# Feeding TensorE values of the chain between the layers of a four-layer graph network

## The chip, the cores and the metric

The kernel runs on one core of one Trainium2 chip, as one launch; the host only transposes some inputs. The metric is the device time of the launch in microseconds. The engines are TensorE (PE in the profile, its weight loads PEld), VectorE (DVE), ScalarE (ACT), GpSimd (POOL) and SyncE (SP), which issues most DMAs. Each runs its own queue of instructions in order; they wait for one another through semaphores.

## What is computed

A graph of N = 2708 nodes with D = 128 features passes through four layers over one dense-stored adjacency matrix `adj` (2708 x 2708, float32, some 2.4% of it not zero). Each layer adds its output to its input and normalizes the rows:

```python
x = _layernorm(x + _L0_gnn_ref(x, adj, ...))       # messages gelu(s_i + d_j + b), weighted by adj; update; layernorm
x = _layernorm(x + _L1_gnn_ref(x, adj, adj, ...))  # sigmoid gates of q k^T, times adj twice; update; layernorm
x = _layernorm(x + _L2_gnn_ref(x, adj, ...))       # hyperbolic: distances of all pairs, attention, exp and log maps
x = _layernorm(x + _L3_gnn_ref(x, adj, ...))       # swish(adj x W + b), twice
```

All arithmetic that matters here is in float32. A float32 matmul is two passes of PE, so two weight loads and two matmul records in the profile.

## The kernel before, in words

Rows of x are kept in 22 tiles of 128 rows (the last has 20), as `x[128, 22, 128]` in SBUF. The four layers follow one another, and each depends on all rows of the one before it.

**Layer 0** (to 880 us) works through blocks of neighbours: PE picks their messages (L817, L822), ACT takes the gelu (L895), DVE weighs (L882), PE adds up (L833). The order is written out by hand under `manual_schedule`, which keeps every engine's instructions in the order of the program. Its tail is what the change touches: `U.sums(n)` multiplies a group of four tiles by the update weights (L863), DVE adds the rest (L864), ACT takes the gelu (L865); `U.rows(n)` adds x (L870) and takes statistics (`moments`, L208). When n is 2, the eight last `far_sum` steps run: DVE adds eight weighted tiles into one tile `extra`, in place (L795). Then `U.norm.all(between)` normalizes twice: `begin` computes mean and scale of 11 tiles from the statistics (`normalizer`, small values of 11 columns), and `shift` applies them on ACT (L246); `add` scales h in place on DVE (L265), adds x (L266) and takes statistics again; `end` shifts x. This goes in two runs of 11 tiles, `early` and `late`; `between` does the last two groups of layer 0, of one tile each.

**Layer 1** (to 1175 us) makes transposed products first (L1042 to L1067), then gates and sums for all pairs of tiles (L1098 to L1105), then an update by groups, then `norm.all_but_end()`: both `begin`, both `add`, and the normalizer of all 22 tiles, whose shift is left to later layers.

**Layer 2** prepares (L1186 to L1298): PE transposes x (L295) and multiplies it (L1211); then comes a long chain on values of 128 x 22, one number for each row of x, made by the helper class `Values` (`tt`, `ts`, `act`, `recip`; L140 to L161); from its results ACT and DVE build X (L1260, L1261), PE transposes it (L1263) and further tables (L1289). This part isn't under `manual_schedule`: the scheduler of the framework orders it by the order of the program and by when operands are ready. Then come all pairs of tiles in trios (L1335 to L1393), for two halves of the columns.

**The end of layer 2 and layer 3** are again written out by hand. `end(1)` and `end(0)` finish layer 2 for tiles 11 to 21 and 0 to 10, each a chain of DVE and ACT with small values of 11 columns and 128-column steps (`each`, L1513). Both take their transposes first; then end(1) runs to its end, then end(0). Layer 3's `neighbours` multiplies x by rows of the adjacency matrix (L1634), first the 11 tiles of end(1), beginning with tile 21 of 20 rows, so PE works while end(0) runs. A second `neighbours` on the result ends the kernel.

Before and after these places PE has real work; within them it waits for DVE and ACT. PSUM has eight banks; the pools of layer 0 (`p_misc`, `p_slot`, `p_out`) take all, and layer 2's preparation takes seven.

Of the kernel before, what the change touches and what calls it, by code (L numbers as in the profile page):

```python
# [20 lines left out]
P = 128  # L21
# [18 lines left out]
def gnn_stack(ctx: ExitStack, tc: tile.TileContext, t, out: bass.AP):  # L40
# [64 lines left out]
    def groups():  # L105
# [4 lines left out]
        return g  # L110

    class Values:

# [24 lines left out]
        def tt(self, a, b, op):  # L138
            o = self.new(a)
            nc.vector.tensor_tensor(o, a, b, op=op)  # L140
            return o

# [6 lines left out]
        def ts(self, a, s1, op0, s2=None, op1=ALU.bypass):  # L149
            o = self.new(a)  # L150
            nc.vector.tensor_scalar(o, a, s1, s2, op0=op0, op1=op1)
            return o

        def act(self, a, func, **kw):
            o = self.new(a)
            nc.scalar.activation(o, a, func, **kw)
            return o

        def recip(self, a):
            o = self.new(a)  # L160
            nc.vector.reciprocal(o, a)  # L161
            return o

# [41 lines left out]
    def moments(st, src, a, b):  # L205

        for i in range(a, b):
            nc.vector.bn_stats(out=st[:, i, :], in_=src[:, i, :])  # L208

    def normalizer(st, a, b, V, sq=None, into=None):  # L210


        even, odd, m2, m5 = (st[:, a:b, k] for k in (1, 4, 2, 5))

        def stt(in0, scalar, in1, op0, op1):
            o = V.new(in0)
            nc.vector.scalar_tensor_tensor(o, in0, scalar, in1, op0=op0, op1=op1)
            return o


        d = V.tt(even, odd, ALU.subtract)
        q = stt(d, 1.0 / 16.0, d, ALU.mult, ALU.mult)
        if sq is None:
            m = stt(m2, LN_EPS * D, m5, ALU.add, ALU.add)
            w = stt(m, 0.25 / D, q, ALU.mult, ALU.add)
        else:
            m = V.tt(m2, m5, ALU.add)
            var = stt(m, 0.25 / D, q, ALU.mult, ALU.add)
            w = V.ts(var, 0.25 * LN_EPS, ALU.add)

        root = V.act(w, AF.Sqrt)
        both = V.tt(even, odd, ALU.add)
        r, off = into or (V.new(d), V.new(d))
        nc.vector.reciprocal(r, V.add(root, V.mul(w, V.recip(root))))
        nc.vector.scalar_tensor_tensor(off, both, -0.5, r, op0=ALU.mult, op1=ALU.mult)
        if sq is not None:
            nc.vector.scalar_tensor_tensor(sq[:, a:b], var, 4.0 * D, V.mul(r, r), op0=ALU.mult, op1=ALU.mult)
        return r, off

    def shift(dst, src, a, b, by, turns="va"):  # L240

        r, off = by
        for i in range(a, b):
            c = slice(i - a, i - a + 1)
            if turns[i % len(turns)] == "a":
                nc.scalar.activation(dst[:, i, :], src[:, i, :], AF.Identity, bias=off[:, c], scale=r[:, c])  # L246
            else:
                nc.vector.tensor_scalar(dst[:, i, :], src[:, i, :], r[:, c], off[:, c], op0=ALU.mult, op1=ALU.add)

    def normalize(dst, src, st, a, b, V, sq=None):  # L250
        shift(dst, src, a, b, normalizer(st, a, b, V, sq))

    class Resnorm:
# [18 lines left out]
        def all(self, between=lambda: None):  # L272
# [4 lines left out]
            self.begin(*late)  # L277
            self.end(*early, "v")
            self.add(*late)
            self.end(*late)  # L280

# [137 lines left out]
    with ExitStack() as l0:  # L419
# [10 lines left out]
        with ExitStack() as msg:  # L430
# [174 lines left out]
            class Rows:  # L605
# [183 lines left out]
                def far_sum(self, k):  # L789
# [4 lines left out]
                    else:  # L794
                        nc.vector.scalar_tensor_tensor(self.extra, f, w, self.extra, op0=ALU.mult, op1=ALU.add)  # L795

                def turn(self):
# [82 lines left out]
            with tc.manual_schedule():  # L880
# [34 lines left out]
                for n in range(ahead):  # L915
# [5 lines left out]
                    if n == 2:  # L921
                        for step in far_sums:
                            step()
                for step in last_turn:
# [21 lines left out]

                U.norm.all(between)

# [67 lines left out]
    def layers_1_to_3(top, before_end=lambda: None):  # L1016

        with ExitStack() as l1:
# [55 lines left out]
            with ExitStack() as att:  # L1074
# [49 lines left out]
                with tc.manual_schedule():  # L1124
# [24 lines left out]
                    look(len(banks) - 1)  # L1149
                    norm.all_but_end()  # L1150

# [9 lines left out]
        with ExitStack() as l2:  # L1161
# [27 lines left out]
            with ExitStack() as pre:  # L1189
# [18 lines left out]
                for n, (a, b, r) in enumerate(together):  # L1208
# [4 lines left out]
                    for i in range(a, b):  # L1213
                        nc.vector.bn_stats(out=st[:, i, :], in_=M[:, i, :D])
                My, Ml, Mr = (M[:, :, D + k] for k in range(3))
                yy, yl, yr = (yw[:, k:k + 1] for k in range(3))
# [253 lines left out]
        with ExitStack() as l3:  # L1470
# [27 lines left out]
            def end(hf):  # L1498
# [11 lines left out]
                def each(dst, src, v, other):  # L1510

                    for i in range(n):
                        nc.vector.scalar_tensor_tensor(dst[:, i, :], src[:, i, :], v[:, i:i + 1], other[:, i, :],  # L1513
                                                       op0=ALU.mult, op1=ALU.add)

                def squares(src):
# [103 lines left out]

            def neighbours(src, order, have, at_end, then, meanwhile, when=0):


                acc = [pacc.tile([P, b - a], F32, name=f"acc{k}") for k, (a, b) in enumerate(banks)]
                swish = Swish(acc, then)
# [47 lines left out]
            with tc.manual_schedule():  # L1673
                nc.sync.dma_start(out=VT0, in_=v_tab)
                for j in near1 + near0:
                    kept[j] = fetch(j, held.tile([P, N], F32, name=f"held{j}"))
                ends = [end(1), end(0)]
                for e in ends:
                    next(e)
                for e in ends:  # L1680
                    for _ in e:
                        pass

                def more():
# [5 lines left out]
                assert sorted(order) == list(range(NT))  # L1690
                first = neighbours(x, order, kept, 3, keep, more, len(far1 + near1) - 1)
                back = (far1 + far0)[::-1]
# [44 lines left out]
```

## Time and profile before

| | |
|---|---|
| device time, three runs | 1918.69, 1918.76, 1921.46 us (median 1918.76) |
| span of the profiled execution, first to last instruction | 1917.7 us |
| PE, DVE, ACT, POOL busy | 1659.6, 1542.7, 1132.0, 680.1 us |
| mean granted TensorE clock | 0.930 |
| matmul records, weight loads | 13973, 13973 |
| last sums of layer 0 to first gates of layer 1 | 880.6 to 955.3 us |
| last update of layer 1 to layer 2's last table | 1171.5 to 1242.6 us |
| last sums of layer 2 to first product of layer 3 | 1615.6 to 1672.4 us |

The profile is of one execution, whose own time lies about 1 us over its span. "PEclk" is the clock that the throttle granted to TensorE, 1.00 being full speed. A timeline row gives start, duration, engine, line, operation, output and inputs, the shape, how many instructions were merged into the row, and in brackets the engine's idle time before it with what ended it. A window's row gives, for each engine, its busy time and the number of its instructions in that stretch, then the clock, the share of the DMA engines and their GB/s. A busy PE is one with a matmul in flight; it says nothing of how much of the array works.

### The profile page before, as it was taken

Reading aid. Unit: us, or ns where it says so; the run is one execution under the profiler, and the core shown is the slowest. Engines: PE = TensorE matmul, PEld = TensorE weight load, DVE = VectorE, ACT = ScalarE, POOL = GpSimd, SP = SyncE. Lnnn points to the kernel's source line nnn. Section 1 sums busy time; section 2 is a strip of 40 time slices with the busy share of each in tenths; the row PEclk is TensorE's granted clock in tenths of the full one; section 3 lists DMA queues with packets and bytes.
Section 4 is the critical chain, followed back from the end, with each engine's and each line's share of the span. In section 5 each row is a group of like instructions: output and inputs, shape, how many; then the busy total and the mean of one; then the engine's idle time right before and its main releaser. Section 6 shows DMA issues by size and latency. Waiting matters only on the chain.

```text
span 1917.7 us, 36464 instructions
## 1 busy us (share of the span) xinstructions
PE 1659.6 (87%) x13973; PEld 949.3 (50%) x13973; DVE 1542.7 (80%) x3632; ACT 1132.0 (59%) x1581; POOL 680.1 (35%) x426
## 2 busy tenths in 40 slices
PE   5899999999999999885699996689998996199995
PEld 4666666666666666664444443322222322044542
DVE  7899999999999999986588885789999997760104
ACT  3566666667666666654344444599998994440003
POOL 5667757767766776664100000022000243000000
PEclk8899999999999999997799997779998997599997
DMA  8756566665666666443044410122222212453330
GB/s 223 161 117 148 121 140 143 132 143 119 148 127 133 146 128 142 91 103 109 1 151 149 170 63 1 61 91 91 78 80 70 98 63 120 161 203 145 139 127 31
DMA packets 218839, 223.63 MB, mean 117 GB/s; under 512 B 28389, under 2 KB 204875, under 8 KB 212067
## 3 DMA queue, kind: packets, MB, share of 16 engines
q1 hardware_dynamic: 167614, 197.53, 33.1%
q0 software_dynamic: 51040, 23.68, 10.5%
q8 instruction: 111, 1.82, 0.4%
q14 instruction: 74, 0.60, 0.1%
HBM read 213.33 MB, written 7.83 MB: 115 GB/s over the span
## 4 chain that ended last, share of the span: by engine, by line
DVE 37%; PE 32%; POOL 10%; issue 7%; ACT 7%; DMA 6%; SPq 0%; DVEq 0%; ACTq 0%; POOLq 0%
PE acc L1634 10%; POOL far L781 9%; PE lg L1098 5%; PE acc L1105 5%; DVE ix L777 5%; DMA far<-d_tab,ix 3%; DVE w L1375 3%; DVE u L1361 3%; DVE m L1364 3%; DVE W L882 3%; PE sl L817 2%; DVE extra L795 2%; DVE m L1381 2%; DVE o L739 2%; DVE m L1378 2%
## 5 line engine op out<-in xcount | busy, mean ns | idle before, releaser
L781 POOL DMA_INDIRECT far<-d_tab,ix x352 | 562.3, 1597 | 259.5 <-DVE W L882 110.8
L895 ACT ACTIVATE g<-sl 128x768 f32<-128x768 f32 x484 | 393.4, 813 | 259.0 <-PE sl L822 240.5
L817 PE MATMUL sl<-dA,S 124*128 124x153 f16 x4840 | 409.0, 232 | 10.4 <-DVE W L882 8.0
L817 PEld LDWEIGHTS <-S 124*128 124x128 f16 x4840 | 331.0, 98 | 80.0 <-issue 68.4
L833 PE MATMUL acc<-g,W 128*32 128x128 f32 x4840 | 206.2, 278 | 0.5 <-DVE W L882 0.5
L1335 POOL TENSOR_TENSOR at<-at,off 128x128 f32<-128x128 f32 (+1 forms) x22 | 71.2, 3249 | 328.8 <-DMA at<-in_adjT 301.2
L833 PEld LDWEIGHTS acc<-g,W 128*32 128x32 f32 x4840 | 140.9, 109 | 58.7 <-issue 54.6
L822 PE MATMUL sl<-s,same 50*128 50x384 f16 x968 | 162.0, 308 | 0.0
L1391 PE MATMUL accV<-m,X 128*128 128x512 f32 (+4 forms) x264 | 128.4, 628 | 33.5 <-DVE m L1381 29.1
L882 DVE TENSOR_TENSOR W<-sl,own 128x150 f32<-128x150 f32 x484 | 143.1, 299 | 14.5 <-ACT g L895 14.2
L1099 ACT ACTIVATE w<-lg,row_L_gnn_gate_bias 128x512 f32<-128x512 f32 (+1 forms) x132 | 83.5, 636 | 108.2 <-PE lg L1098 106.9
L1343 PE MATMUL ps<-XT 128*128 128x512 f32 (+4 forms) x264 | 143.9, 629 | 3.8 <-ACT m L1348 3.6
L707 DVE TENSOR_SCALAR S<-rk 124x1000 f16<-124x1000 bf16 (+1 forms) x330 | 133.4, 430 | 0.0
L777 DVE FIND_INDEX8 ix<-v,o 128x8 uint32<-128x2728 f32 x44 | 131.7, 2993 | 0.0
L316 DVE TENSOR_TENSOR g<-ps,row_L_gnn_b 128x512 f32<-128x512 f32 (+2 forms) x14 | 7.9, 574 | 148.3 <-PE ps L314 148.2
L1098 PE MATMUL lg<-qT,mT 128*128 128x512 f32 (+2 forms) x264 | 121.1, 547 | 3.6 <-ACT w L1099 3.1
L1105 PE MATMUL acc<-w,both 128*128 128x512 f32 (+2 forms) x264 | 121.2, 547 | 0.0
L795 DVE SCALAR_TENSOR_TENSOR extra<-far,v,extra 128x128 f32<-128x128 f32 x330 | 114.8, 348 | 6.3
L739 DVE SCALAR_TENSOR_TENSOR o<-ps,ar 128x496 f32<-128x496 f32 x132 | 82.4, 624 | 38.1 <-PE ps L728 31.7
L1634 PE MATMUL acc<-at,x 128*128 128x512 f32 (+2 forms) x156 | 66.2, 574 | 48.8 <-ACT x L246 48.8
L1100 DVE TENSOR_TENSOR w<-w,at 128x512 f32<-128x512 f32 (+1 forms) x132 | 82.5, 625 | 27.2 <-ACT w L1099 27.1
L1391 PEld LDWEIGHTS accV<-m,X 128*128 128x128 f32 (+1 forms) x264 | 52.1, 211 | 97.0 <-issue 57.7
(358 smaller groups left out, 2697.6 us busy)
## 6 DMA issues: line engine op xcount, KB each, us to landing
at<-in_adjT SPq DMA_DIRECT2D x42, 1354.0 KB
ar<-in_adj SPq DMA_DIRECT2D x105, 248.0 KB
far<-s_tab SPq DMA_DIRECT2D x44, 512.0 KB
at<-in_adjT SPq DMA_DIRECT2D x42, 448.0 KB
at<-in_adjT SPq DMA_DIRECT2D x21, 704.0 KB
at<-in_adjT SPq DMA_DIRECT2D x21, 650.0 KB
held<-in_adjT SPq DMA_DIRECT2D x7, 1354.0 KB
at<-in_adjT SPq DMA_DIRECT2D x21, 280.0 KB
```

The lines of the kernel that those rows point to most:

```text
L777: nc.vector.max_index(ix, self.v[:, n * 8:n * 8 + 8], self.o.rearrange("p b j -> p (b j)"))
L781: nc.gpsimd.indirect_dma_start(out=self.far[n][:, k, :], out_offset=None, in_=d_tab[:, :], in_offset=bass.IndirectOffsetOnAxis(ap=self.ix[ ...
L795: nc.vector.scalar_tensor_tensor(self.extra, f, w, self.extra, op0=ALU.mult, op1=ALU.add)
L817: nc.tensor.matmul(group[c], self.S[h][:, n, c, :], dA[q][:, b, c, :], start=c % 3 == 0 and q == 0, stop=False)
L822: nc.tensor.matmul(out, same[p], self.s3[p, :e - a, :], start=False, stop=True)
L833: nc.tensor.matmul(self.acc[q:q + 32, k, :], W[:, c, :], g[:, c, :], start=b == 0 and k == 0, stop=ends)
L882: nc.vector.tensor_tensor(W[:, :, :RG].rearrange("p (k c) i -> p k c i", k=2), columns_of(sl, D, DA), own[:, None, None, :].to_broadcast([ ...
L895: nc.scalar.activation(g.rearrange("p (k c) d -> p k c d", k=2), columns_of(sl, 0, D), AF.Gelu, scale=1.0 / D_SCALE)
L1098: nc.tensor.matmul(lg, mT[:, j * P:j * P + r], qT[:, a:b], start=True, stop=True)
L1105: nc.tensor.matmul(acc[k], mrow[:rows[j], j, :], ws[j][:rows[j], a:b], start=j == 0, stop=j == NT - 1)
L1391: nc.tensor.matmul(accV[:, a:b], X[:self.r, self.j, :], self.m[:, a:b], start=first, stop=last)
L1634: nc.tensor.matmul(acc[k], src[:rows[j], j, :], at[:rows[j], a:b], start=j == order[0], stop=j == order[-1])
```

## The change

A helper `touch(o)` follows most small steps: if a scratch place is open, PE multiplies the 128 x 128 identity by the value just made, into PSUM that nobody reads. `awake(ps)` opens such a place for a stretch of the program; `awake(None)` closes it for one. Nothing that the output needs is changed. A touch reads its value, so what later writes the same place must wait until the touch is done, and it stands in PE's queue where the program puts it.

```diff
@@ helpers
+    scratch = []
+
+    @contextmanager
+    def awake(ps):
+        scratch.append(ps)
+        yield
+        scratch.pop()
+
+    def touch(o):
+        if scratch and scratch[-1] is not None:
+            nc.tensor.matmul(scratch[-1][:, :o.shape[1]], ident, o, start=True, stop=True)
+        return o
@@ class Values: tt, ts, act and recip
-            return o
+            return touch(o) if len(o.shape) == 2 else o
@@ moments
             nc.vector.bn_stats(out=st[:, i, :], in_=src[:, i, :])
+            touch(st[:, i, :])
@@ normalizer: stt
-            return o
+            return touch(o)
@@ shift
+            touch(dst[:, i, :])
@@ Resnorm.all
             between()
             self.begin(*late)
-            self.end(*early, "v")
-            self.add(*late)
-            self.end(*late)
+            with awake(None):
+                self.end(*early, "v")
+                self.add(*late)
+                self.end(*late)
@@ far_sum
                         nc.vector.scalar_tensor_tensor(self.extra, f, w, self.extra, op0=ALU.mult, op1=ALU.add)
+                    touch(self.extra)
@@ tail of layer 0
                     if n == 2:
-                        for step in far_sums:
-                            step()
+                        with awake(p_out.tile([P, PB, D], F32, name="acc")[:, 0, :]):
+                            for step in far_sums:
+                                step()
...
-                U.norm.all(between)
+                with awake(p_out.tile([P, PB, D], F32, name="acc")[:, 0, :]):
+                    U.norm.all(between)
@@ tail of layer 1
-                    norm.all_but_end()
+                    with awake(acc[0][:, :P]):
+                        norm.all_but_end()
@@ layer 2, after the products of x and to the end of its preparation
+                psum_t = pre.enter_context(tc.tile_pool(name="ps_pre2t", bufs=1, space=PSUM))
+                pre.enter_context(awake(psum_t.tile([P, P], F32, name="scratch")))
@@ each, in end(hf)
                         nc.vector.scalar_tensor_tensor(dst[:, i, :], src[:, i, :], v[:, i:i + 1], other[:, i, :],
                                                        op0=ALU.mult, op1=ALU.add)
+                        if i % 2:
+                            touch(dst[:, i, :])
@@ before layer 3
+                acc = sums_of()
                 ends = [end(1), end(0)]
                 for e in ends:
                     next(e)
-                for e in ends:
-                    for _ in e:
-                        pass
+                with awake(acc[0][:, :P]):
+                    for _ in ends[0]:
+                        pass
+                for _ in ends[1]:
+                    pass
...
-                first = neighbours(x, order, kept, 3, keep, more, len(far1 + near1) - 1)
+                first = neighbours(x, order, kept, 3, keep, more, len(far1 + near1) - 1, acc)
```

`sums_of()` makes the PSUM banks that `neighbours` made itself before; the first call now gets them from outside, since their first bank is also the scratch place. `each` is touched for every second tile, 5 of 11.

More of the change, by code (lines that the diff above doesn't have):

```diff
@@ L2 @@
 import math
-from contextlib import ExitStack
+from contextlib import ExitStack, contextmanager
 import numpy as np
@@ L151, in ts @@
             nc.vector.tensor_scalar(o, a, s1, s2, op0=op0, op1=op1)
-            return o
+            return touch(o) if len(o.shape) == 2 else o
         def act(self, a, func, **kw):
@@ L156, in act @@
             nc.scalar.activation(o, a, func, **kw)
-            return o
+            return touch(o) if len(o.shape) == 2 else o
         def recip(self, a):
@@ L161, in recip @@
             nc.vector.reciprocal(o, a)
-            return o
+            return touch(o) if len(o.shape) == 2 else o
         def sqrt(self, a):
@@ L217, in stt @@
             nc.vector.scalar_tensor_tensor(o, in0, scalar, in1, op0=op0, op1=op1)
-            return o
+            return touch(o)
         d = V.tt(even, odd, ALU.subtract)
@@ L1619, in rows, with sums_of, neighbours @@
                         self.then(a, b, r, g, gate)
-            def neighbours(src, order, have, at_end, then, meanwhile, when=0):
-                acc = [pacc.tile([P, b - a], F32, name=f"acc{k}") for k, (a, b) in enumerate(banks)]
+            def sums_of():
+                return [pacc.tile([P, b - a], F32, name=f"acc{k}") for k, (a, b) in enumerate(banks)]
+            def neighbours(src, order, have, at_end, then, meanwhile, when=0, acc=None):
+                acc = acc or sums_of()
                 swish = Swish(acc, then)
```

## The prediction

> **What bounds the kernel now.** I read the page's second part first (busy tenths and the granted clock by slices), then the chain that ended last, then the windows and the timeline of the three stretches between the layers.
>
> ```profile
> PE   5899999999999999885699996689998996199995
> ...
> PEclk8899999999999999997799997779998997599997
> ...
> DVE 37%; PE 32%; POOL 10%; issue 7%; ACT 7%; DMA 6%; SPq 0%; DVEq 0%; ACTq 0%; POOLq 0%
> ```
>
> TensorE (PE) is busy nearly everywhere but in slices 19 to 20, 25 to 26 and 34 to 35, which lie between the layers (one slice is 47.9 us), and there its clock is down. The chain is DVE's in those stretches and PE's around them. So the change can win only where PE still has a low clock and is the one waited for, and it can lose wherever PE, which takes its instructions in order, gets real work later.
>
> Fine windows show the clock to be 1.0 or 0.5, with changes only at multiples of 3.413 us from each other: down at 888.18, up at 925.74, down at 1209.04, up at 1226.10, down at 1625.46, up at 1686.90. What decides is not busy time. The first tile of the last layer shows it:
>
> ```profile
> 1672.35 9.36 PE L1634 MATMUL acc<-at,x 20*128 20x512 f32 x12 [48.83 <-ACT x L246]
> ```
> ```profile
> 1676.68:1680.09 3.41, 3.41 (x5) 1.33 (x4) 1.91 (x6) 2.11 (x4) 0.00 (x0) 0.50 0.00 0
> 1680.09:1683.50 3.41, 3.41 (x6) 1.50 (x5) 1.09 (x2) 3.41 (x11) 0.00 (x0) 0.50 0.26 60
> 1683.50:1686.91 3.41, 3.41 (x5) 1.35 (x4) 2.92 (x15) 1.69 (x4) 0.00 (x0) 0.50 0.83 346
> 1686.91:1690.33 3.42, 3.42 (x11) 1.73 (x10) 2.48 (x11) 1.38 (x1) 0.00 (x0) 1.00 0.00 0
> ```
>
> PE is busy throughout, yet the clock came up only after the first window that held 128-row matmuls alone; the 20-row tile bought nothing. I gave every matmul pass its columns times two (float32) times rows/128, and added up by window: windows above 2950 such units are followed by 1.0, windows below by 0.5, in 556 of 565; weight loads, if added, make the fit worse. One touch is two passes: 512 units for a 128-column tile, 88 for 22 columns, 44 for 11, 24 for 6. So six wide touches in a window hold the clock; a run of small ones at any rate that PE reaches does not.
>
> The Trainium skill ("TensorE: Matmul & The Clock Gate", Part 1) says that a window of some 3.4 us of busy PE releases the clock and an idle one takes it back. The window's length agrees with the 3.413 us above; by that rule the busy PE at 1672 would have had its clock by 1679.2 at the latest, where the row has 1686.9. By the page the small touches would hold the clock, and the sum would be that of the second rival below.
>
> **What is added.** Nothing is removed. I count, from the helpers, 61 touches after layer 0 (8 far sums, 2 x 9 normalizer values, 2 x 11 shifted tiles, 13 statistics), 73 after layer 1, 97 in layer 2's preparation (71 before the first transpose of X, 26 after it), 124 in end(1): 355, or 710 records of PE. No DMA, DVE or ACT instruction is added.
>
> *Price of a touch on PE.* Nearest rows are a float32 pair with 128x128 weights and few columns. L804 (32 columns):
>
> ```profile
> 867.70 0.41 PE L804 MATMUL ps<-fold,agg 64*128 64x32 f32 x2
> ```
> ```profile
> 891.67 0.50 PEld L804 LDWEIGHTS ps<-fold,agg 64*128 64x128 f32 x2 [0.22 <-ACT o L865]
> 891.67 0.63 PE L804 MATMUL ps<-fold,agg 64*128 64x32 f32 x2
> ```
>
> The first is at full clock, the second at half. Their two passes start 0.133 and 0.235 us apart, the two loads 0.107 and 0.165. So a small touch takes 0.21 to 0.27 us at full clock and 0.33 to 0.47 at half; I take 0.38 at half, the middle, and 0.45 for a wide one (cold 131-column passes of L1211 follow each other by 0.22 at 1198.9). DVE makes such values faster: from 1206.6 to 1221.0 it ran 90 instructions and ACT 11, and 71 of the results are touched, one per 0.20 us.
>
> **Layer 0 to 1.** Here touches make DVE wait. Each far sum rewrites the tile that the touch before it reads, so DVE must wait for PE seven times. That hop is in the trace:
>
> ```profile
> 886.85 3.44 DVE L795 SCALAR_TENSOR_TENSOR extra<-far,v,extra 128x128 f32<-128x128 f32 x8
> ...
> 890.21 0.68 DVE L864 TENSOR_TENSOR o<-o,sl 128x512 f32<-128x512 f32 x1
> ...
> 910.45 0.50 DVE L1044 COPY wT<-ps 128x128 f32<-128x128 f32 x2 [0.63 <-PE ps L1042]
> ...
> 911.01 0.79 PE L1047 MATMUL ps<-wT,wT 128*128 128x128 f32 x2 [0.38 <-DVE wT L1044]
> ...
> 911.84 0.29 DVE L1048 COPY w_qk<-ps 128x128 f32<-128x128 f32 x1
> ```
>
> From DVE's end at 910.95 to its next start at 911.84 are 0.89 us at half clock, for one 128-column pair. At full clock the pair takes some 0.49 (the first of L863, 880.55 to 881.04) and 0.1 of hand-over: 0.59. The sums now start every 0.383 us; with the hop they start every 0.35 + 0.89 (or 0.59): 0.86 (0.55) more each. Two hops fall before 888.2 at full clock, five after: 1.1 + 4.3 = 5.4 us. DVE is the chain there (L795, then L864 at 890.21 without a gap), so nothing covers it. Behind the touches in PE's queue stand the matmuls of sums(3), which ran at 882.6 before and now start after the last touch: 0.5 + 8 x 0.21 + 0.25 = 2.4 us (0.21 a pass, a little under L1211's) that DVE's L864 waits for. Then the scaling of h in place waits for its touch: 0.8. In between(), the last two groups' matmuls (898.1 before, long ready) now stand behind the statistics' touches: DVE waits some 1.0. Sum 9.6. The gain: wide touches of begin(late) bring the clock up near 918.9, but DVE runs without a gap over 0.3 us from 920 to 932, so faster transposes give 0.5 at most in the middle, 2.6 (half of the 5.2 us from 920.5 to 925.7) as a bound. The second low stretch, 936.0 to 942.8, follows a wait without touches and stays. I take +9, from +4 (all hops at 0.59, the gain in full) to +12.
>
> **Layer 1 to 2.** Within the normalization the touches come from ACT's 0.39 us steps and are done before DVE rewrites h: nothing. PE's low clock at 1196.1 to 1202.2 can gain up to 3.0 or lose that to late statistics' touches: 0. Then the scalar chain: 10 touches by 1209.0 at full clock, 61 more at 0.38 = 23.2, so PE is free for X at 1232.2, not at 1221.07: 11.2 us late, and DVE stops at its first copy of XT. After that come 26 further touches, 9.9 us, for a PE that was busy 18.94 of the 22 us from 1221 to 1243; with some overlap and an earlier clock I add 2. I take +13. Below: touches at 0.21 end at 1221.5, and half of the 5.6 cold us from 1230.7 to 1236.3 and the 3.0 above come back: -5. Above, at 0.47: 16.3 + 12.2 = +29.
>
> **Layer 2 to 3.** A full tile takes 4.54 us of PE at full clock (1688.89 to 1693.43). The first two took 9.29 and 7.25, so the low clock costs 7.5 there, and PE is idle for 0.6 us in all from 1672.4 to 1870: that is the prize. But the last 73 touches of end(1) arrive from 1655.9 on, all ahead of the first product: 37 small at 0.38, 5 wide, 20 small, 11 wide: 14.1 + 2.3 + 7.6 + 5.0 = 29, so 1684.9 instead of 1672.35: 12.5 late. The 11 wide ones raise the clock, the 20-row tile loses it again (see above), so about 6 of the 7.5 come back. I take +6.5; from -7 (no backlog, the whole prize) to +12 (0.47 each: 18 late). The touched end(1) chain itself waits for nothing: it writes a touched place again only long after. end(0) runs beside PE and is done by 1720; its first tile is needed after eleven others, at 1684.9 + 11 x 4.5 = 1734.
>
> **Sum.** 9 + 13 + 6.5 = 28.5 on a span of 1917.7 in the profiled execution; the median of the runs shown is 1918.76, 1.1 above the span, which I keep: 1947. Of the bounds, +4 - 5 - 7 = -8 and +12 + 29 + 12 = +53.
>
> **Rivals.** First, *only the hops count*: PE swallows the small touches at DVE's own rate because weight loads run ahead; no backlog and no clock won. For it: loads only 0.107 apart at full clock. Against: 0.165 at half. Price: layer 0's +9, so 1928. Second, the other side, *the clock holds*: if the gate counts the touches as work, then they run at 0.21, as fast as DVE's values come, and PE enters layer 3 at 1.0: 7 there, 5 in layer 2, against +4 to +6 in layer 0: -7, so 1912. It decides as soon as a small touch stays below the 0.20 us that DVE takes for its value; the 20-row tile speaks against it. Third, *nothing moves*: gains and hops cancel, 1918. Fourth, a backlog at 0.47 throughout: 1971.
>
> **Chances.** About 0.2% (3.8 us) is what a measurement of this kernel can tell from none. Backlog 0.50 (1947, own range 1932 to 1966), hops only 0.15, clock holds 0.20, nothing 0.10, heavy backlog 0.05: faster 0.20, same 0.10, slower 0.70. The range 1910 to 1968 leaves about 0.1 below and 0.08 above.
>
> **What would show it.** Right: L795's steps 0.9 to 1.3 us apart with PE as their releaser; PE busy from 1206 with touches at 0.5 clock while the first transposes of X start 10 us after their input; the first L1634 over 8 us after the last shift of end(1). Wrong: a clock of 1.0 through the scalar chains, a touch under 0.2 us, or far sums that keep their 0.38.

## The result, and the profile after

The changed kernel takes 1977.11 us (median of 4 runs, 1970.61 to 1978.22) beside 1919.15 for the kernel before on the same chip: a ratio of 1.029, 95% interval 1.0273 to 1.0306. That is 58 us slower where 28 were forecast, and above the range. The profiled execution has a span of 1976.5 us (58.8 over that of before; its own time is 1978.22), 14683 matmul records, 710 more, as counted, and a mean granted clock of 0.921, which is lower than before. Two of the later runs of the kernel before took 2692 and 2696 us at a mean granted clock of 0.55; they are left out of every comparison.

From the page of the changed kernel, TensorE's busy tenths, its clock, and the chain that ended last:

```profile
PE   5899999999999999887899999989998996899995
...
PEclk8899999999999999995999997579998997589997
...
PE 38%; DVE 37%; POOL 8%; issue 7%; ACT 6%; DMA 4%; DVEq 0%; ACTq 0%; SPq 0%; POOLq 0%
```

TensorE is now nearly as busy between the layers as within them (slices 25 and 35), and its clock is no better there. PE's share of the chain grew from 32 to 38%.

Layer 0's tail, VectorE's timeline of the changed kernel:

```profile
888.75 0.35 DVE L812 SCALAR_TENSOR_TENSOR extra<-far,v,extra 128x128 f32<-128x128 f32 x1 [0.95 <-PE acc L123]
889.99 0.35 DVE L812 SCALAR_TENSOR_TENSOR extra<-far,v,extra 128x128 f32<-128x128 f32 x1 [0.89 <-PE acc L123]
...
899.14 0.69 DVE L882 TENSOR_TENSOR o<-o,sl 128x512 f32<-128x512 f32 x1 [2.59 <-PE sl L881]
```

The far sums (L795 before, L812 now) follow each other by 1.24 us where it was 0.38, TensorE's touch releases each, and VectorE then waits another 2.59 us for the next group's sums. The scaling of h in place waited 1.71 us for ScalarE before; now it waits 3.16 us for a touch, so 1.45 more:

```profile
902.86 0.69 DVE L265 TENSOR_TENSOR o<-o,row_L_gnn_ln_w 128x512 f32<-128x512 f32 x1 [1.71 <-ACT o L246]
```
```profile
913.25 0.69 DVE L281 TENSOR_TENSOR o<-o,row_L_gnn_ln_w 128x512 f32<-128x512 f32 x1 [3.16 <-PE acc L123]
```

Layer 1 to 2: two rows of TensorE's timeline in the kernel before, and then the timeline and one window of the changed kernel (the columns of a window are those of the windows before the change):

```profile
1184.89 1.12 PE L295 MATMUL ps<-ident,x 128*128 128x128 f32 x4 [10.94 <-DVE x L266]
...
1221.07 1.99 PE L1263 MATMUL ps<-ident,X 128*128 128x128 f32 x6 [15.47 <-DVE X L1261]
```

```profile
1207.43 6.55 PE L123 MATMUL acc<-st,ident 128*128 128x6 f32 x44
1213.83 4.87 PE L123 MATMUL acc<-v,ident 128*128 128x22 f32 x22
1218.76 4.74 PE L312 MATMUL ps<-ident,x 128*128 128x128 f32 x21
...
1229.12 25.67 PE L123 MATMUL scratch<-w,ident 128*128 128x22 f32 x142
1254.62 1.31 PE L1286 MATMUL ps<-ident,X 128*128 128x128 f32 x5
```
```profile
1239.40:1242.80 3.40, 3.40 (x18) 3.40 (x17) 2.81 (x17) 0.77 (x2) 0.00 (x0) 0.50 0.00 0
```

Layer 2's transposes of x (L312, before L295) began at 1184.89, beside the additions. Now they stand behind 22 statistics and 11 normalizer touches. Then 71 touches of 22 columns run until X's transposes (L1286), 33.55 us later than before. From 1234.44 to 1282.22 us the grant is 0.5 in all 14 windows of the clock, though TensorE is busy for 45.7 of these 47.8 us; the first six windows (to 1254.9) are busy throughout, with small touches alone but for their last 0.3 us. 22 passes of the normalizer took 4.87 us at half clock. Start to start they are 0.213 us apart, so 0.43 a touch. 22 passes of a wide touch took 4.73 us just before (1202.86 to 1207.59), 0.213 apart as well: at half clock 6 to 22 columns cost as much as 128. The same 22-column passes were 0.112 us apart while the clock was still up (1229.12 to 1234.44): 0.22 a touch.

VectorE's three rewritings of a touched value, in the same kernel's timeline:

```profile
1236.91 0.19 DVE L204 COPY_PREDICATED w<-w,w 128x22 f32<-128x22 uint32 x1 [4.28 <-PE scratch L123]
...
1274.40 0.19 DVE L204 COPY_PREDICATED w<-w,w 128x22 f32<-128x22 uint32 x1 [5.79 <-PE scratch L123]
...
1713.42 0.18 DVE L204 COPY_PREDICATED v<-v,v 128x11 f32<-128x11 uint32 x1 [7.20 <-PE acc L123]
```

`artanh_over` makes f, which is touched, and puts the series into it in place (`copy_predicated`, L190 before). So VectorE waits until TensorE's queue has come to f's touch. In the kernel before VectorE runs the same three without a wait:

```profile
1212.76 0.19 DVE L190 COPY_PREDICATED w<-w,w 128x22 f32<-128x22 uint32 x1
...
1233.01 0.17 DVE L190 COPY_PREDICATED w<-w,w 128x22 f32<-128x22 uint32 x1
...
1660.29 0.17 DVE L190 COPY_PREDICATED v<-v,v 128x11 f32<-128x11 uint32 x1
```

Layer 2 to 3, TensorE:

```profile
1720.84 4.70 PE L123 MATMUL acc<-st,ident 128*128 128x6 f32 x22
1725.40 3.99 PE L123 MATMUL acc<-v,ident 128*128 128x11 f32 x18
1729.24 4.39 PE L123 MATMUL acc<-x,ident 128*128 128x128 f32 x22
1733.56 6.81 PE L1662 MATMUL acc<-at,x 20*128 20x512 f32 x12
```

The first product (L1634 before) starts at 1733.56, 61.2 us late, of which 42.85 were there when layer 2's last table was made. ScalarE's last shift had ended at 1725.40. The wide touches raise the clock at 1732.78, the 20-row tile loses it from 1736.2 to 1743.02.

So the 58.8 us of span came in four parts: +15.9 until layer 1's first gates, +27.0 from there to layer 2's last table, +18.35 to layer 3's first product, -2.4 after it. The forecast's terms for the same four were 9, 13, 12.5 and -6.

### The profile page after: what moved, and what is told of

It is laid out like the page before. It is cut to its first block, busy times and chain, and to the rows that moved or that the text cites. A ratio compares the mean times of both kernels' runs of the same rounds, so it can differ in the third digit from the quotient of the medians.

```text
span 1976.5 us, 37880 instructions
## 1 busy us (share of the span) xinstructions
PE 1800.3 (91%) x14683; PEld 1090.2 (55%) x14683; DVE 1543.9 (78%) x3632; ACT 1132.8 (57%) x1582; POOL 679.0 (34%) x426
## 4 chain that ended last, share of the span: by engine, by line
PE 38%; DVE 37%; POOL 8%; issue 7%; ACT 6%; DMA 4%; DVEq 0%; ACTq 0%; SPq 0%; POOLq 0%
PE acc L1662 10%; POOL far L798 7%; DVE ix L794 5%; PE lg L1118 5%; PE acc L1125 5%; PE acc L123 4%; DVE W L900 3%; DVE w L1398 3%; DVE u L1384 3%; DVE m L1387 3%; PE sl L835 3%; DMA far<-d_tab,ix 2%; DVE extra L812 2%; DVE o L756 2%; DVE m L1404 2%
## 5 line engine op out<-in xcount | busy, mean ns | idle before, releaser
L851 PEld LDWEIGHTS acc<-g,W 128*32 128x32 f32 x4840 | 140.6, 109 | 59.1 <-issue 55.2
L1414 PE MATMUL accV<-m,X 128*128 128x512 f32 (+4 forms) x264 | 124.4, 612 | 35.5 <-DVE m L1404 32.7
L812 DVE SCALAR_TENSOR_TENSOR extra<-far,v,extra 128x128 f32<-128x128 f32 x330 | 115.1, 349 | 12.4 <-PE acc L123 6.3
L763 DVE MAX8 cand<-o 128x8 f32<-128x248 f32 x242 | 90.3, 411 | 0.0
```

The source lines that it names most:

```text
L851: nc.tensor.matmul(self.acc[q:q + 32, k, :], W[:, c, :], g[:, c, :], start=b == 0 and k == 0, stop=ends)
L1414: nc.tensor.matmul(accV[:, a:b], X[:self.r, self.j, :], self.m[:, a:b], start=first, stop=last)
```

## The experiments

The table gives how many us later than in the kernel before each landmark starts in the profiled execution, and the change of the median time beside runs of the kernel before on the same chip. Two executions of the same program differ by 1 to 2 us at such a landmark (the kernel before itself ran from 1913.06 to 1921.46 us), so single differences of that size are not read.

| | layer 1's first gate | x's last transpose (layer 2) | X's first transpose | last table | layer 3's first product | layer 3's last product | time |
|---|---|---|---|---|---|---|---|
| changed | 15.9 | 25.6 | 33.6 | 42.9 | 61.2 | 59.1 | +58.0 |
| only_l0 | 15.6 | 15.6 | 15.5 | 13.3 | 14.8 | 14.8 | +13.5 |
| only_l1 | 1.4 | 9.5 | 4.7 | 4.9 | 4.9 | 4.9 | +3.4 |
| only_l2 | 0.0 | 0.0 | 15.5 | 26.2 | 26.5 | 28.2 | +26.8 |
| only_end | 0.9 | 0.9 | 1.0 | 1.1 | 16.4 | 12.4 | +10.1 |
| no_far | 4.8 | 12.6 | 21.5 | 28.6 | 47.0 | 44.8 | +43.6 |
| free_f | 14.5 | 22.3 | 31.2 | 35.6 | 52.2 | 48.4 | +46.4 |
| wide_only | 8.6 | 8.6 | 8.8 | 8.9 | 10.9 | 5.5 | +5.4 |
| swap | 8.7 | 13.6 | 11.3 | 14.1 | 18.7 | 14.9 | +17.0 |
| tiny | 9.8 | 16.4 | 12.1 | 11.2 | 15.7 | 15.7 | +14.7 |

### Each place alone

In each kernel three of the four places are closed. For only_l1, for example:

```diff
-                        with awake(p_out.tile([P, PB, D], F32, name="acc")[:, 0, :]):
+                        with awake(None):
                             for step in far_sums:
...
-                with awake(p_out.tile([P, PB, D], F32, name="acc")[:, 0, :]):
+                with awake(None):
                     U.norm.all(between)
...
-                pre.enter_context(awake(psum_t.tile([P, P], F32, name="scratch")))
+                pre.enter_context(awake(None))
...
-                with awake(acc[0][:, :P]):
+                with awake(None):
                     for _ in ends[0]:
```

> Touches only in layer 0's tail (the eight far sums and the two normalizations); all other touches are out. Theory (each place costs by itself what the changed kernel's trace shows there): layer 1's gates start some 16 us late, nothing else changes, so +16, about 1935. Rival (the places disturb one another, by shifting the phase of the clock's windows, and alone each costs what the prediction gave it): +9, about 1928.

Measured: 1933.55 us, ratio 1.0067 (1.005 to 1.0084).

> Touches only in the normalization at the end of layer 1 (statistics, normalizers, 22 shifted tiles, onto the first accumulator). Theory: the late statistics' touches stand in TensorE's queue ahead of layer 2's transposes of x, which start only when add is done instead of beside it: +8, about 1927. Rival (the prediction's nothing): 1919.

Measured: 1923.37 us, ratio 1.002 (1.001 to 1.003). TensorE's timeline of only_l1 shows the queue that does it, and that it costs less than its length:

```profile
1198.35 4.91 PE L123 MATMUL acc<-v,ident 128*128 128x22 f32 x22
1203.32 4.35 PE L312 MATMUL ps<-ident,x 128*128 128x128 f32 x21
```

Of the lateness in the table 1.4 us were there before. The transposes of x end 8.1 us later than that, but X is only 3.3 late: the scalar chain works for a while on the row norms, before it needs the transposes' products. My 8 was too much here, and the rival's nothing too little.

> Touches only in layer 2's preparation. Theory: 28.6 us were lost from layer 1's end to layer 2's pairs in the changed kernel, some 8 of them by layer 1's own touches, so +20 here, about 1939; TensorE at 0.5 for over 30 us; VectorE stops 4 to 6 us at each copy_predicated that rewrites a touched value. Rival (the prediction's size): +13, about 1932.

Measured: 1946.78 us, ratio 1.0141 (1.0124 to 1.0158): +26.8, more than the theory's 20. VectorE stops 6.19 and 5.79 us at the two copy_predicated here.

> Touches only in the end of layer 2 for the first run of tiles. Theory: first products of layer 3 some 15 us late, some 4 of the clock's 7.5 won back, so +12, about 1931. Rival (the prediction's size): +6.5, about 1926. The four parts together should give +58 if each place costs by itself what the changed kernel's trace shows, and +28 if the rest comes from the places disturbing one another.

Measured: 1930.13 us, ratio 1.0051 (1.0034 to 1.0068). The first product is 15.3 us late beside the last table, and 4.0 come back by the last product.

The four add up to 53.8 of the changed kernel's 58.0 us. Each place costs by itself most of what its trace showed; the rival, that the places disturb one another, falls. The 4 us that are left are within the uncertainty of the sum.

### Layer 0's sums, and wide touches alone

```diff
 # no_far
-                        with awake(p_out.tile([P, PB, D], F32, name="acc")[:, 0, :]):
+                        with awake(None):
                             for step in far_sums:
 # wide_only
-        if scratch and scratch[-1] is not None:
+        if scratch and scratch[-1] is not None and o.shape[1] == P:
```

> The changed kernel without the touches of the eight far sums; all others stay. Theory: seven hops of 1.24 instead of 0.38 us (6.0) and the late matmuls of sums(3) (2.6) go: -8.6, about 1968. Rival (the sums' wait only hides a later one, the half-clock transposes of layer 1 stay late by the other touches): -3, about 1974.

Measured: 1963.60 us, ratio 1.0231 (1.0214 to 1.0248), 13.5 less than the changed kernel. VectorE's timeline of no_far has the eight sums in one row again, as before the change (L882 follows at 890.01):

```profile
886.65 3.44 DVE L812 SCALAR_TENSOR_TENSOR extra<-far,v,extra 128x128 f32<-128x128 f32 x8
```

At VectorE's last such addition in layer 0 (909.49 in the kernel before) the two kernels differ by 9.1 us, which is the theory's 8.6 (6.0 for the hops, 2.6 for the late matmuls); at the gates by 11.1, at the end by 14. The rest was gained later, and no run says by what.

> The changed kernel with the 128-column touches alone: all small ones (statistics, normalizers, scalar chains) are out. Theory (small touches are load on TensorE and no work to the clock gate): what is left is layer 0's hops, some +11, and a clock that is up at layer 3's start but lost again to the 20-row tile, some -2: about 1928, with no stall at copy_predicated. Rival (the wide ones cost as well, each 0.45 us in TensorE's queue ahead of real work): over 1940.

Measured: 1925.35 us, ratio 1.0034 (1.0022 to 1.0047). The small touches are some 52 of the 58 us, and layer 2's preparation loses nothing without them (8.6 to 8.9 in the table). In layer 0 they are half: 15.9 with, 8.6 without. At layer 3 the wide ones even win: first product 2.0 us later, last product 3.4 us earlier, both beside the last table.

### The rewritten value

```diff
-            f = self.mul(self.ts(a, 0.5, ALU.mult), r)
+            half = self.ts(a, 0.5, ALU.mult)
+            with awake(None):
+                f = self.mul(half, r)
             nc.vector.copy_predicated(f, m.bitcast(U32), p)
```

> The changed kernel, but the value f that copy_predicated rewrites in place is not touched (three touches fewer of 355). Theory: VectorE's stalls there (4.3, 5.8 and 7.2 us) vanish, but TensorE's queue is the bound, so VectorE stops later instead, at XT's first copy and at the shift before layer 3: -5, about 1972. Rival (the rewriting is the loss that the prediction missed): all 17.3 us come back, about 1960.

Measured: 1966.38 us, ratio 1.0249 (1.0223 to 1.0274), 10.7 less than the changed kernel: between the two. All three stalls are gone. Of the first little came back (X's first transpose is only 2.3 us earlier, and 1.4 of that were there at the gates): VectorE waits for the queue at XT's first copy instead (13.65 us, 8.26 in the changed kernel). The second came back nearly in full (the last table is 7.2 us earlier), and of the third some 1.8: TensorE's queue is still there, and VectorE stops again where the shift rewrites a touched x in place. From VectorE's timeline of free_f:

```profile
1709.72 2.05 DVE L265 TENSOR_SCALAR x<-x,v,v 128x128 f32<-128x128 f32 x5 [2.56 <-PE acc L123]
```

### What a small touch costs, and what the clock counts

Each of the two kernels has one of the two marked lines.

```diff
         if scratch and scratch[-1] is not None:
-            nc.tensor.matmul(scratch[-1][:, :o.shape[1]], ident, o, start=True, stop=True)
+            n = o.shape[1]
+            if n < P:
+                nc.tensor.matmul(scratch[-1][:n, :P], o, ident, start=True, stop=True)          # swap
+                nc.tensor.matmul(scratch[-1][:n, :n], o, ident[:, :n], start=True, stop=True)   # tiny, in its place
+            else:
+                nc.tensor.matmul(scratch[-1][:, :n], ident, o, start=True, stop=True)
```

> The changed kernel with the operands of each small touch exchanged: the small value is the weight (6 to 22 columns loaded) and the identity streams, 128 columns a pass instead of 6 to 22. As many touches, as many values waited for. Theory (the gate counts streamed columns times rows, the small touch's price was its weight load): the clock stays at 1.0 through the scalar chains, a touch takes 0.21 to 0.25 us there, TensorE follows VectorE nearly without backlog; layer 2's preparation costs some 5 instead of 27, the end of layer 2 -2 instead of +10: about 1940. Rival (the gate counts what is written, or any busy TensorE alike): the clock stays at 0.5, a touch at 0.43, about 1975.

Measured: 1937.02 us, ratio 1.0099 (1.0081 to 1.0117). The touches are as many and wait for the same values, and 40 us are gone. TensorE's timeline and a window of swap, in the scalar chain:

```profile
1217.00 15.45 PE L125 MATMUL scratch<-ident,w 128*22 128x128 f32 x140
1232.38 0.82 PE L1290 MATMUL ps<-ident,X 128*128 128x128 f32 x5
```
```profile
1220.90:1224.30 3.40, 3.40 (x33) 3.18 (x32) 1.55 (x10) 1.51 (x3) 0.00 (x0) 1.00 0.00 0
```

The clock stays at 1.0 from 950.56 to 1237.28 us, through layer 1, the whole normalization and the scalar chain (in the kernel before it fell at 1178.32), and a touch takes 0.22 us (140 passes in 15.45). TensorE was as busy in the changed kernel's window above, at 0.50. What differs is the stream: 512 units a touch instead of 88 or less, so by the prediction's count some 33 x 256 = 8448 units in this window and 18 x 44 = 792 in that one, on either side of its limit of 2950.

> The changed kernel with small touches that are small on both sides: the value (6 to 22 columns) is the weight, and as many columns of the identity stream. Wide touches and far sums as before. Theory (a small touch's price was the load of 128 weight columns, and its stream is too short for the gate): the clock stays at 0.5 through the scalar chains, as in the changed kernel, but a touch takes under 0.2 us there, so no backlog: far sums and hops remain, +15, about 1935. Rival (each pass costs some 0.22 us at half clock whatever its columns, or the lost time was the low clock itself): about 1975.

Measured: 1934.19 us, ratio 1.0081 (1.0066 to 1.0096). Here the clock is as low as in the changed kernel, and the time is 43 us lower all the same. TensorE's matmuls and weight loads in tiny, and a window of the scalar chain:

```profile
1226.90 4.68 PE L125 MATMUL scratch<-ident,w 128*22 128x22 f32 x46 [0.22 <-DVE w L169]
1233.14 1.73 PE L1290 MATMUL ps<-ident,X 128*128 128x128 f32 x5 [1.56 <-DVE X L1288]
```
```profile
1226.90 0.15 PEld L125 LDWEIGHTS scratch<-ident,w 128*22 128x22 f32 x2 [0.34 <-DVE w L169]
```
```profile
1224.78:1228.19 3.41, 3.01 (x36) 2.17 (x34) 2.90 (x20) 1.50 (x2) 0.00 (x0) 0.50 0.00 0
```

46 passes took 4.68 us at VectorE's pace, with pauses: 0.20 a touch at half clock, where the changed kernel needed 0.43 for the same value. The window also answers a rival that the expectations don't name, that the clock counts passes: it has 36 at 0.50, where swap's had 33 at 1.00 (in units some 36 x 44 = 1584). X's first transpose stands behind no queue: TensorE was idle for 1.56 us before it, until VectorE had made X. So the dear part of the touch was the load of 128 weight columns in each pass at half clock: fewer weight columns (tiny) or the full clock (swap, 0.22 a touch) each take the queue away, and the two end within 3 us of each other. Where a touch is cheap, the low clock in itself cost next to nothing in these chains. Of what both keep, 15 to 17 us, layer 0 has 9 to 10 by the table; the other two places have 1 to 5 each, and no run divides these between waits and wide touches.

### Layer 3's start

The last group asks whether the prize that the prediction saw there, 7.5 us of half clock, can be had at all. order_only has no touches:

```diff
         far1 = [j for j in range(HT, NT) if j not in near1][::-1]
+        far1 = far1[1:] + far1[:1]
...
-                order = (in_turns("fhfhfhfhfhf", h=near1, f=far1)
+                order = (in_turns("hfhfhfhfhff", h=near1, f=far1)
```

> The kernel before, no touches; only the order of layer 3's first eleven tiles: it begins with tile 11, whose shift is done first, and the 20-row tile is the eleventh. Theory (the 20-row tile kept the clock down): first product 2.1 us earlier, and after at most two of the clock's windows at half speed the clock is up, where 14.5 us were half speed before: -2.1 and -2 to -4, about 1914. Rival (the time at half speed is set by something else, or the second half's chain waits anyway): -2, about 1918.

Measured: 1915.12 us, ratio 0.9983 (0.9975 to 0.9992). TensorE's timeline of order_only:

```profile
1669.41 6.18 PE L1635 MATMUL acc<-held,x 128*128 128x512 f32 x12 [46.90 <-issue]
```

Beside the last table the first product starts 1.9 us earlier, and the clock is up at 1672.24, after 2.8 us of half speed where it was 14.5. How long that lasts depends on where the clock's window stands: up to two windows by the rule, here less than one. The 20-row tile takes its toll later instead: the clock is at 0.5 from 1720.03 to 1726.86, and again from 1836.08 to 1839.50, since the order of the second `neighbours` is made from the same list and moves too (the edit does not stay within the first eleven tiles, as its expectation has it). In all, layer 3's start and that tile cost 13.1 us at half speed, where the start cost 14.5. So of the gain of 4.3 us some 1.9 are the earlier start and some 0.7 the clock (half of the 1.4 us, an estimate); what the rest is, no run says.

late_swap adds touches, late_swap_old_order has the same touches and the order of before. In these and the three kernels after them the touches of all other places are out:

```diff
-                each(x[:, own, :], uh, V.mul(V.mul(th, c), V.shrink(th)), x[:, own, :])
-                moments(st, x, a, b)
-                yield
-                normalize(x, x, st, a, b, V)
+                v = V.mul(V.mul(th, c), V.shrink(th))
+                with awake(idle):
+                    each(x[:, own, :], uh, v, x[:, own, :])
+                    moments(st, x, a, b)
+                    by = normalizer(st, a, b, V)
+                shift(x, x, a, b, by)
```

> The order of order_only, and touches only in the last step of the end of layer 2 (five wide ones, statistics and normalizer with the small value as weight and the identity streaming), none on the shifted tiles. Theory (27 touches of 512 units in 7 us hold the clock, cost under 0.25 us each and are done when the first tile is shifted): layer 3 begins 2 us earlier and at 1.0: -9.6, about 1910. Rival (they stand in front of the first product, or the gap to it loses the clock again): no better than the order alone, 1914 or more.

Measured: 1916.83 us, ratio 0.9987 (0.9978 to 0.9996).

```profile
1666.95 4.38 PE L125 MATMUL acc<-ident,st 128*6 128x128 f32 x22
1671.17 2.13 PE L125 MATMUL acc<-ident,v 128*11 128x128 f32 x18
1673.23 4.81 PE L1669 MATMUL acc<-held,x 128*128 128x512 f32 x12
```

TensorE's timeline of late_swap says why the theory's 1910 wasn't reached: the touches began cold, so each took 0.4 us, and they were done 2 us after order_only would have started. The clock was won (up at 1670.7), the start was lost; the rival holds here.

> The same touches with the order of before, the 20-row tile first. Theory (rows count): the tile starts at full clock, loses it for one or two windows, which costs 2 to 3 of the 7.5 us: about 1914. Rival (once up, a busy TensorE keeps its clock): -7.5, about 1912, no window at 0.5 after the first product.

Measured: 1916.06 us, ratio 0.9985 (0.9976 to 0.9994). TensorE begins at 1.0 and is busy, and still the clock is down from 1678.08 to 1684.92, behind the 20-row tile. The theory's window is there, the rival (a busy TensorE keeps its clock) falls. The time is that of late_swap within the noise: with the touches in front, the order no longer matters. TensorE's timeline and two windows:

```profile
1673.79 5.17 PE L1668 MATMUL acc<-at,x 20*128 20x512 f32 x12
1678.89 7.79 PE L1668 MATMUL acc<-held,x 128*128 128x512 f32 x12
```
```profile
1674.67:1678.08 3.41, 3.41 (x9) 1.48 (x8) 3.31 (x10) 0.00 (x0) 0.00 (x0) 1.00 0.00 0
1678.08:1681.50 3.42, 3.42 (x6) 1.51 (x5) 1.92 (x6) 2.03 (x3) 0.00 (x0) 0.50 0.50 139
```

early_swap starts the touches earlier and ends them before the normalizer, early_ident is the same with the identity as the weight, early_swap_free_f leaves f untouched as above:

```diff
+                with awake(idle):
                     m = V.ts(V.mul(both[:, 0, :], c), TINY, ALU.max)
                     s = V.shrink(m)
...
                     moments(st, x, a, b)
+                by = normalizer(st, a, b, V)
+                shift(x, x, a, b, by)
```

> The order of order_only; touches with the small value as weight (identity streaming) from the last scalar chain of the end of layer 2 to the statistics, none on the last normalizer or on the shifted tiles. Theory (the gate counts streamed columns times rows, at full clock such a touch takes 0.22 us, as long as VectorE needs for its value): the clock is up by some 1662 and stays, all touches are done before tile 11 is shifted, layer 3 begins at 1669 to 1670 at 1.0: about 1911, 4 below order_only. Rival (the gap of 2 us after the last touch loses the clock, or copy_predicated's wait makes the chain late): no better than order_only, 1915 or more.

Measured: 1916.57 us, ratio 0.9983 (0.9974 to 0.9992), no better than the order alone. The clock is up at 1661.5 and stays until 1726.36, as the theory says, but VectorE stopped for 3.45 us at f, since the first touches, to 1661.5, ran at half clock and left a queue. That is the rival's second half:

```profile
1665.61 0.18 DVE L208 COPY_PREDICATED v<-v,v 128x11 f32<-128x11 uint32 x1 [3.45 <-PE acc L125]
```

> The same kernel with the touches as the changed kernel has them: identity as weight, small value streaming. Same values, same number, same place in TensorE's queue. Theory (128 weight columns loaded a pass, no work to the gate): clock 0.5 through the chain, 0.44 us a touch, some 37 small ones from 1655 on plus 16 behind them end near 1680, the first product 10 us late: about 1925. Rival (only the order of operands differs, a touch is a touch): within 3 us of early_swap.

Measured: 1931.13 us, ratio 1.0062 (1.005 to 1.0074). The touches end at 1681.25 and the clock is down until 1685.9. The roles of the operands alone are worth 14.6 us here, where the expectations had 14; both kernels lie 6 us above theirs, and both wait at f (7.22 us in this one).

> early_swap with one touch less: the value f that copy_predicated rewrites in place is not touched. Theory (the wait of 3.45 us at copy_predicated set the start of layer 3, since TensorE at full clock keeps pace and has next to no backlog to put in its place): nearly all of it comes back, layer 3 begins 2.5 to 3.4 us earlier at 1.0, about 1914. Rival (TensorE's backlog takes its place, as it did for most of the stalls in free_f): under 1 us, 1916.

Measured: 1911.71 us, ratio 0.9962 (0.9948 to 0.9977), 4.9 less than early_swap and the fastest of all. TensorE's timeline:

```profile
1652.93 10.87 PE L125 MATMUL acc<-ident,v 128*11 128x128 f32 x72 [32.64 <-DVE v L158]
1663.73 1.38 PE L127 MATMUL acc<-x,ident 128*128 128x128 f32 x10
1665.04 2.57 PE L125 MATMUL acc<-ident,st 128*6 128x128 f32 x22
1667.54 4.81 PE L1669 MATMUL acc<-held,x 128*128 128x512 f32 x12
```

VectorE has no stall at f, the clock is up from 1658.78, and layer 3 begins at 1.0, 4.8 us earlier than before (2.2 beside the last table, where early_swap began 1.5 later). Where TensorE keeps pace, the wait of 3.45 us at f was a loss of its own, and it came back whole: 3.8 us beside the last table. So the prize can be had in part. The 20-row tile still takes 10.2 us to half clock at its two new places (1716.81 to 1723.64 and 1832.86 to 1836.28).

## Why the prediction was wrong

The sign, the places and the main mechanism (a backlog of small touches in TensorE's queue that hardly count for the clock) were right; the size was half, and two waits were put at nothing that were there: the one behind layer 1's late statistics and VectorE's at copy_predicated. By its own steps:

- **The clock.** The rule held: what is counted is streamed columns times rows. It was 0.5 for 47.8 us in the changed kernel with TensorE busy for 45.7 of them, 1.0 in swap to the end of the scalar chain (1237.28), and 0.5 again behind the 20-row tile in late_swap_old_order. The rival "the clock holds" fell for these touches. swap shows more: even with the clock held the kernel is 17 us slower, so that rival's 1912 was wrong in its price too. The Trainium skill's rule ("TensorE: Matmul & The Clock Gate", Part 1: a busy window of some 3.4 us releases the clock) has the window's length right; the changed kernel's six windows in a row that are busy throughout, at 0.50, speak against busyness as its measure.
- **The price of a small touch.** 0.38 us, the middle between 0.33 and 0.47, was too low: 0.43 in the long rows, as for a wide one. I took it from L804, a single pair (whose weights have 64 rows, not 128), and a single pair does not show how fast a long row of such passes goes. I had the sign of it in its loads (0.107 and 0.165 us for 128 columns) and did not ask what a load of 128 columns sets as a floor. The same page (Part 2, "LDWEIGHTS (loading the stationary operand)") states that a weight load's time goes with its columns, whatever the rows; the traces agree: passes in a row start 0.04 us apart with 22 weight columns (tiny) and 0.213 apart with 128 (the changed kernel), both at half clock, and in the kernel before a load of 128 columns at L1634 took 0.33 us with 20 rows and 0.34 with 128.
- **Layer 0 to 1.** +9 was forecast, +15.9 measured (13.5 alone, by the medians). Hops 6.0 and the late matmuls of sums(3) 2.6 were forecast at 5.4 and 2.4; that the hop of 0.89 came out is in part luck, since VectorE ran other instructions (L870, L208) between the two rows that I read it from. What failed is the rest: "the scaling of h in place waits for its touch: 0.8" was 1.45 (3.16 before L281 where 1.71 stood before L265), between() 2.0 before its sums where I had 1.0, and layer 1's first weight products (L1062, before L1042), of which I had not thought, stood behind the late run's touches: 2.70 at L1064. wide_only and tiny, 8.6 and 9.8 at the gates, say that these surpluses are the price of the small touches.
- **Layer 1 to 2.** +13 was forecast, +27.0 measured. "Within the normalization ... nothing" failed: the order of TensorE's queue puts the late statistics ahead of the transposes of x, 3.3 us at X in only_l1. "X 11.2 us late" was 15.5 in only_l2, mostly by the price (61 touches at 0.43 instead of 0.38 are 3 of the 4.3 us). The largest miss is "with some overlap and an earlier clock I add 2" for the 26 touches after X: 10.7 in only_l2 (15.5 to 26.2). There was no overlap: the touches stand ahead of the transposes that make the last tables, VectorE waits 5.79 us at the second copy_predicated, and the clock came no earlier.
- **Layer 2 to 3.** 12.5 late and 6 back were forecast; 18.35 late and 2.4 back came (15.3 and 4.0 in only_end). "The touched end(1) chain itself waits for nothing: it writes a touched place again only long after" failed: copy_predicated rewrites f in VectorE's next instruction, 7.20 us. I read the helper's end as a new value. Without it free_f starts 1.8 us earlier here beside the last table, for the queue is still there; over all three places this reading is worth 10.7 us. The price adds some 2.8 us by an estimate (57 small touches at 0.43 instead of 0.38). And the 20-row tile costs more of the prize than I allowed: 6.8 us at half clock behind it (1736.2 to 1743.02) where 14.5 were, so some 3.9 back by an estimate.
- **Sum.** The surplus of 30.3 us in the span is 6.9 + 14.0 + 5.85 + 3.6 (layer 0 to 1, layer 1 to 2, the late start of layer 3, and what came back). The heavy backlog, 0.47 us throughout, gave 1971 and was the nearest of the cases; it had 0.05. That it came near is in part luck: the touch took 0.43, and the waits that it left out make up for the difference.

What stays open: what won no_far 5 us more than the hops and the late matmuls, and whether the 4 us between the four parts and the whole are more than noise.

## What to carry to other kernels

Before feeding an in-order engine with extra work, list what stands behind each piece in its queue and which later instruction writes the piece's place again (in-place helpers such as copy_predicated count): those two lists, and not the engine's idle share, give the price. Here a float32 matmul of few streamed columns under a full-width weight cost its weight load, and making the small operand the weight took away 40 of the 58 us (swap) or 43 (tiny). And raising a clock that is low beside a chain of another engine was worth next to nothing here: the two things that paid were to start with a full tile that is ready first, and touches that end before the first real product.

## What the runs showed of the hardware

- The gate gives weight loads and short streams little weight however busy TensorE is: 0.50 in a window with 3.40 of 3.40 us busy and 18 passes of 22 columns (changed kernel), 1.00 in one as busy with 33 passes of 128 columns (swap), and 0.50 again with 36 passes of 22 columns (tiny). In swap it counts passes whose weights fill only 6 to 22 of the 128 columns, so how much of the array's width is filled is not what it weighs.
- float32 passes under 128 weight columns start 0.213 us apart at half clock whether 6, 22 or 128 columns stream (22 passes took 4.87 us with 22 columns and 4.73 with 128), and 0.112 apart at full clock with 22; with 22 weight columns and 22 streamed, a pair of passes follows VectorE at 0.20 us a touch at half clock.
- A 20-row tile loses a clock that is up: from 1.0 at its start to 0.5 for two windows (1678.08 to 1684.92), with TensorE busy throughout.
